# Expert weights fetched by SyncE with a condition instead of by GpSimd's indirect gather, in a two-layer graph-attention and mixture-of-experts kernel

## The chip, the cores and the metric

The kernel runs on one core of a Trainium2 chip. The metric is device time in microseconds (us) of one launch. The engines of the core are TensorE (PE in the profile; its weight loads are PEld), VectorE (DVE), ScalarE (ACT), GpSimd (POOL) and SyncE (SP). SyncE computes nothing here; it begins transfers and holds registers. Each engine works through its own list of instructions in order; semaphores tie the lists together.

## The reference

Two layers run one after the other on `x` (2708 tokens of 256) with a 0/1 matrix `adj` (2708 x 2708). Each layer is a masked attention over the graph with a residual, and then a mixture of 8 experts with a residual:

```python
x = x + gnn0(layernorm(x), adj)          # softmax of masked q k^T / sqrt(d), then elu
x = x + ffn0(layernorm(x))
x = x + gnn1(layernorm(x), adj)          # additive scores, softmax, alpha @ H
x = x + ffn1(layernorm(x))

# ffn0 (hidden size H = 1024); ffn1 is alike with H = 512 and without the norm of its own
probs = softmax(xt @ Wr + br)
top_p, top_idx = top_k(probs, 2)
weights = top_p / top_p.sum(-1)
xe = norm(xt)[None] * ln_g[:, None] + ln_b[:, None]
h = gelu(einsum('end,edh->enh', xe, W1) + b1[:, None])
y = einsum('enh,ehd->end', h, W2) + b2[:, None]
out = (weights * y[top_idx of each token]).sum(over the two experts)
```

Every token uses two of the eight experts, so 5416 rows go through an expert in each layer. All of it is in float32.

## The kernel before

**Stages.** In the trace the first attention ends at about 545 us, the first FFN at 893, the second attention at 1143, the second FFN at 1397; the last scatters and the copy to the output end at 1420.

**Routing.** While attention produces tiles of 128 tokens, each tile is normed and routed: its rows, with the token's number and its gate value appended, are scattered (L748, GpSimd) to a DRAM tensor `disp` that has a region for each expert.

**Slots.** A slot is 128 rows of one expert's region. There are up to 50 slots in a layer; the last four are behind two conditions, and 46 run in the first FFN and 48 in the second. `place` (L755 to L853) works out on VectorE, from the number of rows that each expert has, for every slot: its expert, the first row in `disp` (`token_row`), and where its weights are (`weight_row`). It is called twice in a layer: for the first 24 slots when 16 tiles have been routed, and for the others once all are. 

**Weights.** All the weights and biases of an expert are one packed tensor of 128 rows, one row for each SBUF partition: 17,456 bytes a row (2.23 MB an expert) in the first layer, 9,232 bytes (1.18 MB) in the second. They go into one of `RING = 4` SBUF buffers, slot s into buffer s % 4. Slots of one expert follow each other, so often the buffer holds the wanted expert already from slot s - 4. `fetch_weights` (L872) is a gather by GpSimd (L874) with one row index for each partition; where the buffer has the expert, `place` adds `FAR` to the index, which is then out of bounds, and the transfer of that row is left out.

**Rows.** `fetch_rows` (L882) loads `token_row` into a SyncE register (L884) and moves 128 rows of `disp` to one of six buffers `xg` (L889).

**The loop.** `slot(s)` (in `slots`, L905) runs `up` and then `down` of the slot before:

- `up`: two transposes `tp` (L913, TensorE) of `xg`; a copy to `xe` on VectorE (L917 twice in the first FFN, where it applies the expert's norm, L923 once in the second); a copy of the second bias (L926); the first matmuls `mm` (L933: 16 of them in the first FFN, 8 in the second); gelu on ScalarE (L941) to `hT`.
- `down`: the second matmuls into `acc` (L949: 8 in the first FFN, 4 in the second); then `fetch()` for slot s + `AHEAD`, with `AHEAD = 3`; then `y` on VectorE (L955 adds the bias, L956 multiplies by the gate); then a scatter-add of `y` to the result `xd` in DRAM by GpSimd (L957). The scatter-adds of one layer stand in a chain: each waits for the one before to land, since a token's two rows come from two slots.

Two `ps_mm`, `ps_tp` and `ps_acc` PSUM buffers each, and two buffers of `xe`, `bias2` and `hT`, let two slots overlap.

**What sets the order.** SyncE's list is in the order of the program (`tc.manual_schedule(engines={SP})`). The lists of all other engines are ordered by the scheduler when the program is built, which takes the instructions of all engines together: `up` and `down` are not in the order in which they are written, and a change on one engine can move instructions on another. A `Line` hands out work of the attention stage's last tiles (norms, routing; L682 writes a tile to `xd`) between the steps of the slots.

Of the kernel before, what the change touches and what calls it, by code (L numbers as in the profile page):

```python
# [15 lines left out]
ALU = mybir.AluOpType  # L16
# [3 lines left out]
P = 128  # L20
# [3 lines left out]
E = 8  # L24
# [23 lines left out]
OFTEN = (46, 48)  # L48
AHEAD = 3
DROW = D + 2  # L50
FAR = 1 << 20
IDLE = E * CAP


# [1 line left out]
def adj_ffn_kernel(ctx: ExitStack, tc: tile.TileContext, a: dict, out: bass.AP):  # L56
    nc = tc.nc
# [31 lines left out]
    part = const.tile([P, 1], F32, name="part")  # L89
# [47 lines left out]
    for c in range(DC):  # L137
# [3 lines left out]
            op0=ALU.mult, op1=ALU.mult, accum_out=wfc[:, c, D : D + 1],  # L141
# [471 lines left out]
    class Experts:  # L613
# [141 lines left out]
        def place(self, s0, s1):  # L755
# [3 lines left out]
            all_chunks = s0 > 0  # L759
# [4 lines left out]
            if all_chunks:  # L764
# [3 lines left out]
                for e in range(E):  # L768
                    at = nc.values_load(
                        end[0:1, e : e + 1], min_val=e * CAP, max_val=e * CAP + N,  # L770
                        engines=(mybir.EngineType.SP,),
                        skip_runtime_bounds_check_because="an expert has at most N tokens",
                    )
# [12 lines left out]
            first = one.tile([P, E], F32, name=f"first{s0}")  # L786
# [12 lines left out]
            passed = one.tile([P, n, E], F32, name=f"passed{s0}")  # L799
# [5 lines left out]
            row = one.tile([P, n], F32, name=f"row{s0}")  # L805
# [32 lines left out]
            same = one.tile([P, SLOTS], F32, name=f"same{s0}")  # L838
            r0 = max(s0, RING)
            if s0 < RING:  # L840
# [4 lines left out]
            )  # L845
            weights = one.tile([P, n], F32, name=f"weights{s0}")
            nc.vector.tensor_scalar(
                weights, self.expert[:, s0:s1], float(P), part[:, 0:1], op0=ALU.mult, op1=ALU.add
            )
            nc.vector.scalar_tensor_tensor(  # L850
                self.weight_row[:, s0:s1], same[:, s0:s1], float(FAR), weights,
                op0=ALU.mult, op1=ALU.add,
            )  # L853

        def begin(self):

# [14 lines left out]

        def fetch_weights(self, s):  # L872
            w, packed = self.ring[s % RING], self.packed_weights[0]
            nc.gpsimd.indirect_dma_start(  # L874
                w, None, packed[:],
                bass.IndirectOffsetOnAxis(ap=self.weight_row[:, s : s + 1], axis=0),
                bounds_check=E * P - 1, oob_is_err=False,
            )
            return w

        def fetch_rows(self, s):
# [198 lines left out]
```

The softmax here doesn't subtract the row's maximum and nothing guards it: scores larger than these inputs give would overflow.

## Time and profile before

The kernel takes 1418.33 us (median of 3 runs, 1415.91 to 1423.79). The profiled execution took 1421.76 us, with a span of 1420.0 us and a mean granted TensorE clock of 0.964.

| what | value |
|---|---|
| FFN slots run, first and second | 46 and 48 |
| gathers of weights L874 | 99, mean 1055 ns of GpSimd |
| scatter-adds L957 | 94, mean 1586 ns of GpSimd |
| row transfers L889 | 99 |
| hardware queue q1 (SyncE) | 107.86 MB, 27.0% of 16 DMA engines' time |
| software queue q0 (GpSimd) | 93.73 MB, 23.0% |
| a slot of the first FFN, steady | 7.28 us |
| a slot of the second FFN, without stalls | 4.34 us |

How to read it: PE, DVE, ACT and POOL with a number of us are busy times of an engine over the span. A matmul in float32 leaves two records in the trace, so L949 x1120 are 560 instructions. In lines of costliest groups, "busy, mean ns | idle before, releaser" follow the bar; in a timeline, the columns are start, length, engine, line, operation, `out<-in`, shapes, and in square brackets the idle time before and what ended it. Ends of matmuls are modelled, so neighbours can seem to overlap by 0.1 to 0.2 us.

### The profile page before, as it was taken

The page shows a single profiled execution, that of the slowest core. Times are in us where ns is not written, and L with a number is a line of the kernel's source. Part 1 is how long each engine was busy: PE and PEld are TensorE (multiplying, and loading weights), DVE is VectorE, ACT ScalarE, POOL GpSimd, SP SyncE. Part 2 cuts the span into 40 slices and gives each one's busy share as a digit, 9 for nine tenths or more (in the row PEclk, how much of TensorE's full clock was granted, in tenths as well). Part 3 has the DMA queues.
Part 4 walks back from the last instruction along what each step waited for, and adds up shares of the span by engine and source line. Part 5 has one row for each costly group of instructions (what it writes and reads, how often), then busy time and mean ns, then how long its engine had stood idle before and what let it go on. Part 6 is the DMA issues. An engine that isn't in the chain of part 4 may idle for free. (4 is left out here: it accounts for less than half of the span.)

```text
span 1420.0 us, 21606 instructions
## 1 busy us (share of the span) xinstructions
PE 1292.1 (91%) x7680; PEld 1009.8 (71%) x7680; DVE 569.7 (40%) x2182; ACT 348.9 (25%) x1035; POOL 435.3 (31%) x478
## 2 busy tenths in 40 slices
PE   5999999999999999999999999599989876989872
PEld 3676666666566666999999999478878565878662
DVE  5623744536417264422221222565465543323220
ACT  2322222122112224433333332232001142222120
POOL 5100110110101122543333333431333346555552
PEclk8999999999999999999999999899999978999996
DMA  7601785978727036556686543310221256564664
GB/s 238 207 4 42 205 203 148 248 181 226 190 71 169 23 132 241 156 169 201 203 297 198 155 123 100 81 32 12 65 79 54 73 177 154 114 170 106 183 185 105
DMA packets 108620, 203.01 MB, mean 143 GB/s; under 512 B 25197, under 2 KB 83861, under 8 KB 101933
## 3 DMA queue, kind: packets, MB, share of 16 engines
q1 hardware_dynamic: 76172, 107.86, 27.0%
q0 software_dynamic: 32336, 93.73, 23.0%
q8 instruction: 63, 1.03, 0.3%
q14 instruction: 49, 0.39, 0.1%
HBM read 261.27 MB, written 69.41 MB: 233 GB/s over the span
## 5 line engine op out<-in xcount | busy, mean ns | idle before, releaser
L949 PE MATMUL acc<-ring,hT 128*128 128x256 f32 x1120 | 279.4, 386 | 24.8 <-ACT hT L941 24.8
L933 PE MATMUL mm<-xe,ring 128*128 128x128 f32 x2240 | 286.0, 283 | 9.7 <-DVE xe L923 4.7
L933 PEld LDWEIGHTS mm<-xe,ring 128*128 128x128 f32 x2240 | 275.9, 198 | 23.9 <-issue 14.0
L941 ACT ACTIVATE hT<-mm,ring 128x128 f32<-128x128 f32 x560 | 159.6, 368 | 376.8 <-issue 292.7
L949 PEld LDWEIGHTS acc<-ring,hT 128*128 128x128 f32 x1120 | 200.0, 192 | 55.9 <-ACT hT L941 34.6
L345 PE MATMUL s<-g,xnT 128*128 128x512 f32 (+1 forms) x440 | 215.2, 605 | 4.9 <-DVE mT L357 4.9
L367 PE MATMUL acc<-v,p 128*128 128x257 f32 (+1 forms) x880 | 216.9, 390 | 0.0
L957 POOL DMA_INDIRECT xd<-y,xg x94 | 149.1, 1586 | 173.5 <-DVE y L955 61.1
L517 PE MATMUL acc<-parts,mT 128*128 128x257 bf16 (+1 forms) x1452 | 175.7, 274 | 1.5 <-POOL parts L504 1.0
L955 DVE TENSOR_TENSOR y<-acc,bias 128x256 f32<-128x256 f32 x94 | 39.8, 424 | 339.1 <-PE acc L949 286.6
L367 PEld LDWEIGHTS acc<-v,p 128*128 128x128 f32 (+1 forms) x880 | 159.7, 192 | 19.2
L517 PEld LDWEIGHTS <-mT 128*128 128x128 fp8e4 (+1 forms) x1452 | 137.4, 98 | 30.6 <-issue 9.7
L748 POOL DMA_INDIRECT disp<-row,to x88 | 86.4, 982 | 235.7 <-DVE to L745 139.2
L874 POOL DMA_INDIRECT ring<-L_ffn_packed,weight_row x99 | 104.4, 1055 | 157.9 <-issue 102.9
L156 POOL TENSOR_TENSOR ln_rs<-ln_rs,minus_half 128x2 f32<-128x2 f32 x88 | 66.8, 779 | 245.9 <-DVE ln_rs L152 198.6
L357 DVE TENSOR_SCALAR mT<-s 128x512 fp8e4<-128x512 f32 x110 | 75.4, 687 | 150.4 <-ACT p L356 149.2
L345 PEld LDWEIGHTS s<-g,xnT 128*128 128x128 f32 (+1 forms) x440 | 77.1, 187 | 58.4 <-issue 45.9
L356 ACT ACTIVATE p<-s 128x512 f32<-128x512 f32 x110 | 65.0, 594 | 192.3 <-PE s L351 192.3
L351 PEld LDWEIGHTS <-apart 128*128 128x128 fp8e4 (+1 forms) x440 | 34.2, 99 | 64.5 <-issue 64.5
L257 DVE TENSOR_SCALAR apart<-adj 128x677 fp8e4<-128x677 int32 x80 | 40.9, 515 | 54.2 <-DMA adj<-in_adj_dram 53.7
L913 PE MATMUL tp<-ident,xg 128*128 128x128 f32 x188 | 39.3, 279 | 20.3 <-DMA xg<-disp 17.2
L166 PE MATMUL misc<-ident,xn 128*128 128x128 f32 (+1 forms) x132 | 27.5, 290 | 23.4 <-DVE ln_rs L152 11.6
(183 smaller groups left out, 1067.7 us busy)
## 6 DMA issues: line engine op xcount, KB each, us to landing
adj<-in_adj_dram SPq DMA_DIRECT2D x84, 338.5 KB
L_ffn_packed<-in_L_ffn_W_dram SPq DMA_DIRECT2D x16, 1024.0 KB
xg<-disp SPq DMA_DIRECT2D x99, 129.0 KB
L_ffn_packed<-in_L_ffn_W_dram SPq DMA_DIRECT2D x16, 512.0 KB
neighbours<-mT SPq DMA_DIRECT2D x5, 1408.0 KB
mT<-neighbours SPq DMA_DIRECT2D x5, 1408.0 KB
xin<-in_x_dram SPq DMA_DIRECT2D x42, 128.0 KB
xd<-x SPq DMA_DIRECT2D x42, 128.0 KB
```

Source lines behind the costliest of these rows:

```text
L156: nc.gpsimd.tensor_tensor(rs[:r, 1], rs[:r, 0], minus_half[:r], ALU.pow)
L345: nc.tensor.matmul(ps[:kr, :nb], xnT[:, c, k0 : k0 + kr], g[:, c, :nb], start=(c == 0), stop=False,)
L356: nc.scalar.activation(p[:kr, :nb], ps[:kr, :nb], AF.Exp, scale=1.0 / 16.0)
L357: nc.vector.tensor_scalar(mT[:kr, k, :], ps[:kr, :nb], -BIG / 2, None, ALU.is_gt, saturate=False,)
L367: nc.tensor.matmul(accs[j][:r], p[:kr, j * P : j * P + r], v[:kr, k, :], start=(k == 0), stop=(k == NT - 1),)
L517: nc.tensor.matmul(acc[:r], mT[:, k, q0 : q0 + r], parts[:, k, i], start=(k == 0 and i == 0), stop=(k == NT - 1 and i == 2),)
L748: nc.gpsimd.indirect_dma_start(disp[:], bass.IndirectOffsetOnAxis(ap=to[:r, j : j + 1], axis=0), rows2[j][:r], None,)
L874: nc.gpsimd.indirect_dma_start(w, None, packed[:], bass.IndirectOffsetOnAxis(ap=self.weight_row[:, s : s + 1], axis=0), bounds_check=E * P ...
L933: nc.tensor.matmul(ps[:, i, :], w[:, c * hidden + f * P : c * hidden + (f + 1) * P], xe[:, c, :], start=(c == 0), stop=(c == DC - 1),)
L941: nc.scalar.activation(hT[:, f, :], ps[:, i, :], AF.Gelu, bias=w[:, b1 + f : b1 + f + 1])
L949: nc.tensor.matmul(ps, hT[:, f, :], w[:, w2 + f * D : w2 + (f + 1) * D], start=(f == 0), stop=(f == hc - 1),)
L957: start = nc.gpsimd.indirect_dma_start(xd[:], bass.IndirectOffsetOnAxis(ap=xg.bitcast(I32)[:, D : D + 1], axis=0), y, None, compute_op=ALU ...
```

## The change

The weights of a slot are fetched by SyncE in place of GpSimd. `place` now writes `weight_row` as twice the first row of the expert in the packed tensor, plus one where the buffer has the expert already (or, in the second call, where the slot is past the last one in use). SyncE loads that number into a register, shifts it for the row, and begins an ordinary transfer of 128 rows with the lowest bit as its condition. The gather, its list of 128 indices and `FAR` go. It is meant to free GpSimd, whose other work in the slots is the chain of scatter-adds, and to take the weights out of GpSimd's software queue. `fetch()` calls `fetch_weights` and then `fetch_rows`, as before, so on SyncE the weights of slot s + 3 now stand ahead of its rows.

```diff
@@ place
             weights = one.tile([P, n], F32, name=f"weights{s0}")
             nc.vector.tensor_scalar(
-                weights, self.expert[:, s0:s1], float(P), part[:, 0:1], op0=ALU.mult, op1=ALU.add
-            )
-            nc.vector.scalar_tensor_tensor(
-                self.weight_row[:, s0:s1], same[:, s0:s1], float(FAR), weights,
-                op0=ALU.mult, op1=ALU.add,
-            )
+                weights, self.expert[:, s0:s1], float(E - 1), float(2 * P), op0=ALU.min, op1=ALU.mult
+            )
+            if all_chunks:
+                nc.vector.tensor_tensor(
+                    same[:, s0:s1], same[:, s0:s1], passed[:, :, E - 1], ALU.max
+                )
+            nc.vector.tensor_add(self.weight_row[:, s0:s1], same[:, s0:s1], weights)
@@ fetch_weights
             w, packed = self.ring[s % RING], self.packed_weights[0]
-            nc.gpsimd.indirect_dma_start(
-                w, None, packed[:],
-                bass.IndirectOffsetOnAxis(ap=self.weight_row[:, s : s + 1], axis=0),
-                bounds_check=E * P - 1, oob_is_err=False,
-            )
+            at = nc.values_load(
+                self.weight_row[0:1, s : s + 1], min_val=0, max_val=2 * (E * P - P) + 1,
+                engines=(mybir.EngineType.SP,),
+                ...
+            )
+            row = nc.s_assert_within(
+                at >> 1, 0, E * P - P,
+                ...
+            )
+            nc.sync.dma_start(w, packed[bass.ds(row, P), :], cond=(at & 1) == 0)
             return w
```

## The prediction

> **What bounds the kernel now.** I read the page first: busy shares, then the 40 slices.
>
> ```profile
> PE 1292.1 (91%) x7680; PEld 1009.8 (71%) x7680; DVE 569.7 (40%) x2182; ACT 348.9 (25%) x1035; POOL 435.3 (31%) x478
> ...
> PE   5999999999999999999999999599989876989872
> ```
>
> TensorE (PE) is at 9 tenths or more nearly everywhere; each slice is 35.5 us. Only slices 31 to 40 (from about 1100 us, the second FFN) have holes. So the change must be judged in two stages with different limits. The windows by stage confirm it (columns: window, length, PE, PEld, DVE, ACT, POOL busy, PE clock, DMA share, GB/s): the first FFN, then the second.
>
> ```profile
> 600.00:700.00 100.00, 100.00 (x690) 92.20 (x689) 20.75 (x65) 31.93 (x112) 35.97 (x28) 1.00 0.63 193
> 700.00:800.00 100.00, 100.00 (x693) 92.12 (x692) 22.11 (x70) 30.78 (x108) 35.08 (x27) 1.00 0.71 231
> ```
>
> ```profile
> 1250.00:1300.00 50.00, 42.83 (x265) 37.16 (x265) 15.45 (x41) 11.85 (x42) 26.07 (x21) 0.97 0.63 172
> ```
>
> The first FFN has no TensorE hole at all: nothing removed from GpSimd can help it, and anything that opens a hole costs its full length. The second has 14% idle. Its waits, PE alone, 1190 to 1405 us (total, times, longest):
>
> ```profile
> PE acc L949 <- ACT hT L941: 24.2, 40, 10.6
> PE tp L913 <- DMA xg<-disp: 8.8, 5, 2.8
> PE mm L933 <- DMA ring<-L_ffn_packed,weight_row: 4.7, 4, 1.4
> ```
>
> The long one is not a wait for gelu alone: all engines stop for some 10 us near 1180. Rows and weights together cost 13.5 us.
>
> What the removed instruction cost GpSimd is in the costliest groups:
>
> ```profile
> L874 POOL DMA_INDIRECT ring<-L_ffn_packed,weight_row x99 | 104.4, 1055 | 157.9 <-issue 102.9
> L957 POOL DMA_INDIRECT xd<-y,xg x94 | 149.1, 1586 | 173.5 <-DVE y L955 61.1
> ```
>
> GpSimd is 31% busy, so these 104 us are not a bound by themselves.
>
> **What hides the transposes.** The timeline of one first-FFN slot on TensorE (start, length, engine, line; 7.28 us from tp to tp):
>
> ```profile
> 853.14 0.38 PE L913 MATMUL tp<-ident,xg 128*128 128x128 f32 x2
> 853.36 1.03 PE L949 MATMUL acc<-ring,hT 128*128 128x256 f32 x4
> 854.22 0.64 PE L933 MATMUL mm<-xe,ring 128*128 128x128 f32 x4
> 854.70 0.60 PE L949 MATMUL acc<-ring,hT 128*128 128x256 f32 x2
> 855.13 3.29 PE L933 MATMUL mm<-xe,ring 128*128 128x128 f32 x28
> ```
>
> The first mm needs xe, which VectorE copies out of tp, and comes 1.08 us after tp's start. Those are filled by two matmuls of the down of the slot before (s, where tp belongs to s+1) (1.03 us; four records, two to an instruction, as everywhere in this trace).
>
> **What the Trainium skill says.** "DMA: Bandwidth & Descriptors", section "Issuing engines are not separate DMA queues", says that DMAs begun by SyncE or GpSimd run on the same 16 engines and interleave, so another issuer saves sequencer time only. The trace agrees as far as it goes: hardware and software queues both do their bytes there (27.0% and 23.0% of 16 engines' time for 107.86 and 93.73 MB, about equal cost a byte). So the moved weights land at about the old rate. Same page, "Latency and other measured facts": first byte after about 600 ns for SyncE's path and 1 us for GpSimd's; the trace shows GpSimd busy 1.055 us for one gather and no first byte. I take 0.4 us saved per transfer, which nothing waits for in steady state.
>
> **The change part by part.**
>
> *GpSimd*: 99 x 1.055 = 104.4 us go. In the first FFN they lie beside a full TensorE: 0. In the second a gather sits between two scatter-adds. Each scatter waits for the one before to land: starts 4.55 to 6 us apart, mean about 5.1 over 40 of them. TensorE's slot is 4.34 us where it doesn't stall (tp at 1240.38, mm from 1242.99, 4.34 or 4.39 apart) but 4.83 on average (slot 7's mm at 1193.71, slot 45's at 1377.33: 183.6/38). This is the relief to be had: at most 38 x (4.83 - 4.34) = 18.6 us, with a few more at both ends.
>
> *SyncE*: per fetch one more register load, two register operations, and a DMA. The trace has a register load at 0.19 us and a row DMA at 0.33 us median, a register operation at 0.04; with a margin for the condition 0.75 us, 99 x 0.75 = 74 us. SyncE has nothing else in the slots but rows, whose wait on a freed xg is 415.6 us in all: hidden. What is new is order. The row's load stands behind the weights, and those wait for the down that frees the ring buffer; but that down is the same point of the program that issued the gather before, and both are wanted three slots later (13 us in the second FFN, over 20 in the first). I take 0, and 10 us as the upper end, for attention's last tiles, whose xd writes stand on the same engine.
>
> *Skipping*: about as many transfers are skipped as now; bytes unchanged: 0.
>
> *VectorE in place*: one operation more, twice a layer, small: under 0.5 us.
>
> *Order of matmuls*: the part that the diff doesn't show. Only SyncE's order is written out; the rest is set when the program is built, and moving 99 instructions off GpSimd changes it. I compared the two built instruction lists on TensorE. Slots of the first FFN:
>
> ```
> before: mm x14 | down(s-1) x5 | tp(s+1) x2 | down(s) x2 | mm(s+1) x2 | down(s) x1 | mm x14
> after:  mm(s) x16 | down(s) x8 | tp(s+1) x2 | mm(s+1) x16
> ```
>
> Before, 41 of 50 boundaries have two downs between tp and the mm that needs it; after, 35 have none, 5 one, 8 two, 2 three. On VectorE y of the finished down now stands ahead of xe, often with the bias copy too. In the second FFN tp stood between mm and down, filling part of the gelu wait (at 1240.38 tp, at 1241.05 down, after 0.29 idle); after, 41 of 50 are mm, down, tp, mm.
>
> Price in the first FFN: with nothing between, TensorE stands from tp's start to the first mm with 1.08 us, of which tp's own 0.2 to 0.38 was paid before; but the downs that filled 1.03 us come elsewhere, so a slot grows by 1.03. With one down between (0.5 us) about 0.6. Where y and both others go first, 0.34 + 0.28 more. Over 46 slots: 0.70 x 46 x 1.07 = 34, plus 5 x 0.6 = 3, plus some 3 for the longer VectorE orders: **+40 us** (30 to 52).
>
> Price in the second: mm start to down start stays 2.46 (1238.59 to 1241.05, gelu ends that), down start to tp 1.83 (1241.05 to 1242.88), then tp to mm: y from 0.20 to 0.62, xe pitched 0.34 behind it and 0.42 long, 0.1 to the matmul, 1.1. Sum 5.4 where it was 4.34 stall-free. The stalls on rows and weights should vanish, since a slot is longer than everything behind it (scatter 4.55). Against 4.83: 38 x 0.57 = 22, less some boundaries with the old order, **+18 us** (0 to 30).
>
> *Ends of the second FFN*: slots 46 and 47 and the last scatters (1394.27, 1399.68, 1404.24) run behind today by two slots; without gathers between them -9. Start: rows arrive beside three gathers and TensorE waits up to 5.46 us at 1139.35; GpSimd stands 11.42 us at 1155.50 before a gather while the last tiles' norm is behind it; -5 of these. **-14 us** (-25 to 0).
>
> Sum: 1418.3 + 40 + 18 - 14 = 1462, taken as 1460.
>
> **Rivals.**
> *GpSimd relief wins* (0.13): the copies' exposure is small, because TensorE's queue runs at a modelled end and weight loads overlap; first FFN +10, second at 4.4 a slot, -16, ends -14: 1398. For: 14% holes in the second FFN; GpSimd 52% busy there against 36% in the first. Against: 1.08 us from tp to mm are measured, and a strict engine order can't fill them.
> *No change* (0.07): half the exposure, 20, against -20: 1418. It needs two errors that cancel.
> *SyncE becomes a second brake* (0.20): the longer VectorE order in all slots (1.6 exposed: 46 x 1.6 = 74 less what is filled, some 60), and rows that wait behind a weight's buffer (+10), gains as above: 1418 + 60 + 10 + 18 - 14 = 1492. For: SyncE's waits can't be passed by what stands behind. Against: three slots of slack.
> *Forecast* (0.60): 1460.
>
> **How the numbers follow.** Faster by over 0.5% is the first rival, 0.13; within, 0.07; slower is the forecast and the last, 0.80. The forecast's own bounds: 1418 + 30 + 0 - 25 = 1423 to 1418 + 52 + 30 - 0 = 1500, ends seldom met together. The range keeps no change (1418) and all but the upper third of the last rival, so it leaves out 0.13 and 0.07: 1416 to 1494.
>
> **What would show it.** First FFN: PE in windows of 100 us falls from 100 to about 88, the slot grows from 7.28 to about 8.3 us, and a wait of mm on xe appears in nearly every slot, some 0.7 us each, for 30 us or more. Second FFN: slot about 5.4 us, waits on xg and ring almost gone, waits on xe up to 30 us. Attention unchanged within 3 us; POOL busy about 331 us. It is wrong if PE in the first FFN stays at 100, or if the second FFN is shorter than its 254 us (1143 to 1397); the SyncE rival is right if waits for rows or ring exceed 20 us.

## The result, and the profile after

The changed kernel takes 1452.97 us (median of 4 runs, 1451.25 to 1455.37) against 1417.12 us for the kernel before on the same chip: 1.0246 times as long, with a 95% interval of 1.0207 to 1.0286. That is 36 us slower; 1460 was forecast. The two profiled executions that are compared below differ by 30 us, since the one before took 1421.76 us, 4.6 more than its median.

The page of the changed kernel, its busy shares and the slices of TensorE:

```profile
PE 1302.6 (90%) x7680; PEld 1011.0 (70%) x7680; DVE 561.9 (39%) x2184; ACT 346.5 (24%) x1033; POOL 327.8 (23%) x379
...
PE   5999999999999999999999999699989977777873
```

GpSimd lost 107.5 us of work, as it was to. TensorE has the same 7680 matmul records; its share hardly moved, and the tenths of the slices are too coarse to show the loss. The windows show it (window, length, then PE, PEld, DVE, ACT, POOL busy, PE clock, DMA share, GB/s), two of the first FFN and one of the second:

```profile
600.00:700.00 100.00, 92.27 (x612) 83.82 (x611) 20.71 (x63) 27.56 (x98) 21.65 (x14) 1.00 0.58 178
700.00:800.00 100.00, 94.29 (x631) 85.66 (x630) 20.82 (x65) 27.64 (x98) 19.69 (x13) 1.00 0.67 210
...
1250.00:1300.00 50.00, 40.32 (x244) 33.73 (x244) 11.25 (x37) 10.92 (x39) 14.03 (x9) 1.00 0.54 143
```

TensorE stood at 100 of 100 us in the first FFN before; now it has 6 to 8 us of holes in 100 and 9 to 11% fewer matmul records in the same time. What ended the holes is in the waits of TensorE, whole run:

```profile
PE mm L938 <- DVE xe L928: 26.3, 38, 1.7
PE mm L938 <- DVE xe L922: 22.5, 30, 1.5
PE acc L954 <- ACT hT L946: 21.5, 40, 1.8
...
PE tp L918 <- DMA xg<-disp: 2.6, 1, 2.6
...
PE mm L938 <- DMA ring<-L_ffn_packed: 1.5, 2, 1.3
```

The two first lines are new in this size: `mm` waits for the copy `xe` in the second FFN (L928, 38 times) and in the first (L922, 30 times). The waits for rows and weights, 17.2 and 4.7 us before, fell to 2.6 and 1.5. One slot of the first FFN on TensorE's timeline has the reason in it:

```profile
879.80 3.84 PE L938 MATMUL mm<-xe,ring 128*128 128x128 f32 x32 [0.62 <-DVE xe L922]
883.48 3.62 PE L954 MATMUL acc<-ring,hT 128*128 128x256 f32 x16
886.93 0.38 PE L918 MATMUL tp<-ident,xg 128*128 128x128 f32 x2
887.93 3.84 PE L938 MATMUL mm<-xe,ring 128*128 128x128 f32 x32 [0.62 <-DVE xe L922]
```

Nothing stands between `tp` at 886.93 and the `mm` at 887.93 that needs its copy. From `mm` to `mm` are 8.13 us where it was 7.28. Of the 45 boundaries between slots of the first FFN, one had `mm` right behind `tp` in the trace before; 30 have it now. Added up by stage, from the first `mm` to the last `acc` of each FFN on TensorE (us):

| stage | before | after | difference |
|---|---|---|---|
| up to the first FFN's first mm | 552.8 | 552.3 | -0.5 |
| first FFN | 340.4 | 367.4 | +27.0 |
| rest of the second attention, to the second FFN's first mm | 250.5 | 245.3 | -5.2 |
| second FFN | 253.7 | 265.2 | +11.5 |
| last scatters and copy | 22.6 | 19.8 | -2.8 |
| span | 1420.0 | 1450.0 | +30.0 |

### The profile page after: what moved, and what is told of

Read it like the earlier page. It is cut to its first block, busy times and chain, and to the rows that moved or that the text cites. A ratio compares the mean times of both kernels' runs of the same rounds, so it can differ in the third digit from the quotient of the medians.

```text
span 1450.0 us, 21996 instructions
## 1 busy us (share of the span) xinstructions
PE 1302.6 (90%) x7680; PEld 1011.0 (70%) x7680; DVE 561.9 (39%) x2184; ACT 346.5 (24%) x1033; POOL 327.8 (23%) x379
## 3 DMA queue, kind: packets, MB, share of 16 engines
q8 instruction: 63, 1.03, 0.3%
## 5 line engine op out<-in xcount | busy, mean ns | idle before, releaser
L938 PE MATMUL mm<-xe,ring 128*128 128x128 f32 x2240 | 278.1, 281 | 50.9 <-DVE xe L928 26.3
L938 PEld LDWEIGHTS mm<-xe,ring 128*128 128x128 f32 x2240 | 262.7, 194 | 71.7 <-DVE xe L928 36.4
L954 PE MATMUL acc<-ring,hT 128*128 128x256 f32 x1120 | 268.2, 386 | 21.7 <-ACT hT L946 21.5
L946 ACT ACTIVATE hT<-mm,ring 128x128 f32<-128x128 f32 x560 | 159.3, 368 | 424.0 <-issue 383.8
L954 PEld LDWEIGHTS acc<-ring,hT 128*128 128x128 f32 x1120 | 204.1, 191 | 54.1 <-ACT hT L946 31.3
L922 DVE TENSOR_SCALAR xe<-tp,ring 128x128 f32<-128x128 f32 x92 | 33.6, 401 | 60.8 <-PE tp L918 60.8
L350 PE MATMUL s<-minus_big,apart 128*128 128x128 bf16 (+1 forms) x440 | 42.8, 220 | 0.0
```

Source lines behind the costliest of these rows:

```text
L350: nc.tensor.matmul(ps[:kr, j * P : j * P + r], apart[:, j, k0 : k0 + kr], minus_big[:, :r], start=False, stop=(j == len(ts_) - 1),)
L938: nc.tensor.matmul(ps[:, i, :], w[:, c * hidden + f * P : c * hidden + (f + 1) * P], xe[:, c, :], start=(c == 0), stop=(c == DC - 1),)
L946: nc.scalar.activation(hT[:, f, :], ps[:, i, :], AF.Gelu, bias=w[:, b1 + f : b1 + f + 1])
L954: nc.tensor.matmul(ps, hT[:, f, :], w[:, w2 + f * D : w2 + (f + 1) * D], start=(f == 0), stop=(f == hc - 1),)
```

## Experiments

Each kernel ran beside the kernel before on the same chip; a time is followed by its ratio to that kernel and, in brackets, the 95% interval of the ratio. Four theories are named in the expectations. **A**: the loss is the order of matmuls that the rebuilt program got. **B**: it is the fetch by SyncE itself. The first four kernels tell these apart, two orders by two ways to fetch. They also brought a result that neither foresaw, and **C** (a weight transfer of SyncE delays the landing of the scatter-add beside it) and **D** (SyncE's instructions and waits do it) are about that.

### Two orders by two ways to fetch

In all four, TensorE's list in the slots is tied down by edges from each of its matmuls to the one before, and `down` is split so that its matmuls are written between or ahead of `up`'s. Nothing else is written differently; the lists of the other engines are again ordered by the scheduler. The comments in the cut are not in the kernels.

```diff
-                hT, bias2 = up(w, xg)
+                xe, bias2 = up_tp(w, xg)                 # tpfirst: tp, down, mm
+                ps = None if behind is None else down_mm(*behind)
+                hT = up_mm(w, xe)                        # downfirst has down_mm ahead of up_tp
 ...
+            def behind_in_list(i):                       # called on every matmul of up and down
+                if pe:
+                    tc.add_manual_dep(i.ins, pe[0].ins.name, ..., reason="order")
+                pe[:] = [i]
```

**The kernel before with the common order of the changed one** (gather_downfirst):

> The kernel before, gathers on GpSimd untouched, with the order of the changed kernel's common slot tied down in all slots: mm(s), down(s), tp(s+1), mm(s+1). Theory A: the loss appears without any change to the fetch: first-FFN slots 8.13 us (46 x 0.85 = +39), second-FFN slots 5.4 us where they averaged 4.83 (+18), stalls on rows and weights gone, start and end as before: about 1470 us. Theory B: within 10 us of the kernel before, 1410 to 1428 us.

Measured: 1485.42 us, 1.0428 of the kernel before (1.0401 to 1.0455), 15 us over the 1470 expected. The first FFN took 383.8 us (+43.4) and the second 290.1 (+36.4). The slots of the second FFN are 5.40 us apart from slot 6 to slot 45, as expected; what is over in this stage lies at its two ends, mostly before slot 7. The gathers on GpSimd were untouched, and the slot has the same hole, as TensorE's timeline shows:

```profile
863.31 0.38 PE L927 MATMUL tp<-ident,xg 128*128 128x128 f32 x2
864.31 3.93 PE L951 MATMUL mm<-xe,ring 128*128 128x128 f32 x32 [0.62 <-DVE xe L932]
```

So the order alone makes a loss of this kind, without the change to the fetch. This is against theory B.

**The changed kernel with that order in all slots** (sync_downfirst):

> The changed kernel with mm(s), down(s), tp(s+1), mm(s+1) in all slots, where the built order has about 7 in 10 of them. Theory A: first-FFN slots all 8.13 us, 46 x 0.85 = 39 against the 29 us lost now, the second FFN as now at 5.40: about 1463 us, and 7 us below the gathers with this order (the start's row waits). Theory B: no more than 3 us from the changed kernel, 1450 to 1456 us.

Measured: 1479.34 us, 1.0399 (1.0369 to 1.0429). The first FFN took 382.6 us, 1 us from the gathers with this order. With this order the fetch makes no difference in the first FFN; the order makes all of it. The time came out 16 us above what was expected. Some 10 us of that lie in the second FFN, which took 275.1 us where the changed kernel has 265.2, and 5 in the first, whose slots took 8.22 us for 8.13; the kernel before took 1423.42 us beside it, 6 us more than beside the changed kernel. Against the gathers with the same order, this second FFN is 15 us shorter. Both kernels take 205 us from slot 7 to slot 45, so SyncE's fetch gains at the ends of the second FFN, as the prediction has it.

**The kernel before with the transposes first** (gather_tpfirst):

> The kernel before, gathers on GpSimd untouched, with mm(s), tp(s+1), down(s), mm(s+1) tied down in both FFNs. It prices the fetch alone against the changed kernel with the same order. Theory A: first-FFN slots stay 7.28 us; the second FFN keeps its stalls for rows and weights and its scatter-adds 5.1 us apart, 4.8 us a slot: 1405 to 1420 us, and 15 to 25 us above the changed kernel with this order. Theory B: at or below the changed kernel with this order.

Measured: 1424.21 us, 0.9998 (0.9977 to 1.002). The first FFN took 340.9 us, the second 259.9. This order and the order built for the kernel before are worth the same in total time. The other half of the expectation was missed: this kernel is 19 us below the changed kernel with the same order, the next one, where theory A had it 15 to 25 us above. On that side theory B was right.

**The changed kernel with the transposes first** (sync_tpfirst):

> The changed kernel, with TensorE's order in the slot loops tied down: mm(s), tp(s+1), all of down(s), mm(s+1), in both FFNs. Theory A, the loss is the order of matmuls that the rebuilt program got: first-FFN slots 7.28 us again (-29 us over the stage), second-FFN slots 4.34 to 4.55 us (down to what the scatter-adds allow, 37 x 0.9 = -33), so about 1391 us, below both kernels, with the waits of mm on xe gone. Theory B, the loss is the fetch by SyncE itself (weights and rows landing later, or SyncE's order): slots stay near 8 and 5.4 us, 1440 to 1455 us, and TensorE waits for ring or xg where it waited for xe.

Measured: 1443.61 us, 1.0135 (1.0109 to 1.0161), some 50 us above what theory A expected. It lies in the range of theory B, but without B's signs: slots of the first FFN didn't stay near 8 us, and TensorE waits 39.8 us for `xe` in the second FFN and only 11.1 for `ring` and `xg`. The first FFN did as theory A said: slots of 7.25 us, 345.5 us in all. TensorE's timeline there:

```profile
872.30 0.38 PE L932 MATMUL tp<-ident,xg 128*128 128x128 f32 x2
872.52 3.62 PE L972 MATMUL acc<-ring,hT 128*128 128x256 f32 x16
875.98 3.73 PE L956 MATMUL mm<-xe,ring 128*128 128x128 f32 x32
```

The second FFN did not: 278.3 us, where the kernel before took 253.7 and the changed one 265.2. From 1195 to 1247 us its slots ran 4.29 us apart, and then between 4.5 and 8 us. In that part VectorE waits like this (its waits, 1245 to 1405 us):

```profile
DVE y L982 <- DMA xd<-y,xg: 118.1, 25, 7.0
```

`y` needs one of three buffers, which an earlier scatter-add has to leave, and while VectorE stands there it makes no `xe` for TensorE: a `tp` of 1268.25 us got its `xe` at 1273.24, behind a `y` that was let go at 1272.31. So the chain of scatter-adds bounds this stage once TensorE is fast. Theory B has a part in it after all, but in a place that the changed kernel doesn't show. GpSimd's timeline of the same kernel:

```profile
1265.58 1.61 POOL L984 DMA_INDIRECT xd<-y,xg  x1 [5.49 <-DVE y L982]
1272.94 1.61 POOL L984 DMA_INDIRECT xd<-y,xg  x1 [5.75 <-DVE y L982]
1280.30 1.61 POOL L984 DMA_INDIRECT xd<-y,xg  x1 [5.75 <-DVE y L982]
1284.85 1.61 POOL L984 DMA_INDIRECT xd<-y,xg  x1 [2.94 <-DVE y L982]
1289.44 1.63 POOL L984 DMA_INDIRECT xd<-y,xg  x1 [2.99 <-DVE y L982]
```

The brackets name `y`, but this `y` is for a later slot, since its second instruction ended only at 1273.12, behind the start of the scatter-add at 1272.94: one landing lets go both the next scatter-add and the `y` that takes the freed buffer. Starts are 7.4, 7.4, 4.6 and 4.6 us apart. The bytes of the hardware queue tell which is which. First the DMA view from 1272.94 to 1280.30, then from 1280.30 to 1284.85 (queue, packets, MB, share of 16 engines):

```profile
q1 hardware_dynamic: 288, 1.31, 54.8%
q0 software_dynamic: 144, 0.13, 11.4%
```

```profile
q0 software_dynamic: 144, 0.13, 27.0%
q1 hardware_dynamic: 144, 0.13, 11.1%
```

In the long interval a weight transfer (1.18 MB) was beside the scatter-add's 0.13 MB; in the short one there were only rows. From 1213 us to the end, 14 intervals are longer than 6 us and sum to 103.7 us, 40 us more than 14 of 4.55 would be. Of the intervals between 1240 and 1410 us, the 13 with a weight transfer in them are 7.1 to 8.3 us, and 14 of the 16 without one are 4.5 to 4.6.

### What delays the scatter-adds

These kernels start from sync_tpfirst.

**No weight transfers in the second FFN after slot 3** (sync_tp_noload):

```diff
+            if self.hidden == 512:
+                nc.vector.memset(same[:, r0:s1], 1.0)
```

> The kernel sync_tpfirst with every weight transfer of the second FFN after slot 3 skipped by its condition (SyncE's instructions stay): it leaves out those weights, so its slots use stale ones. Theory C, a weight transfer begun by SyncE shares the DMA engines with the scatter-add just issued and delays its landing, and the chain of scatter-adds is the bound: scatter-adds 4.5 to 4.6 us apart throughout, no waits of y for landings over 1 us each, 37 us less, about 1406 us. Theory D, SyncE's own instructions or the wait for freed xg buffers slow the chain: starts stay 7 us apart in places and the time within 10 us of sync_tpfirst.

Measured: one run, 1388.48 us beside 1411.94 for the kernel before, 0.983. The second FFN took 230.4 us for 278.3, so 48 us less; 37 less were expected. GpSimd's timeline; from 1230 us on all starts but two are 4.3 to 4.6 us behind the last:

```profile
1271.32 1.55 POOL L986 DMA_INDIRECT xd<-y,xg  x1 [2.96 <-issue]
1275.69 1.55 POOL L986 DMA_INDIRECT xd<-y,xg  x1 [2.82 <-issue]
1280.10 1.55 POOL L986 DMA_INDIRECT xd<-y,xg  x1 [2.86 <-issue]
1284.60 1.55 POOL L986 DMA_INDIRECT xd<-y,xg  x1 [2.95 <-issue]
```

SyncE's loads, shifts and skipped transfers are all still there. So theory D is out as the main cause, and C holds in this: it is the transfer itself that delays the landing.

**Weights in four transfers of a quarter of the columns** (sync_tp_split4):

```diff
-            nc.sync.dma_start(w, packed[bass.ds(row, P), :], cond=(at & 1) == 0)
+            part = self.packed_weights[-1] // 4
+            for c in range(0, 4 * part, part):
+                nc.sync.dma_start(
+                    w[:, c : c + part], packed[bass.ds(row, P), c : c + part], cond=(at & 1) == 0
+                )
```

> The kernel sync_tpfirst with a slot's weights moved as four transfers of a quarter of the columns (2,308 bytes a row in the second FFN, 4,364 in the first, for 9,232 and 17,456). Theory C with sharing packet by packet: a scatter-add's packets wait behind packets a quarter as long, so scatter-adds with a transfer beside them start about 5.5 us apart where it was 7.2, 14 x 1.7 = 24 us less, about 1419 us. If only the bytes in flight count, and not the packets' size: no change, 1438 to 1446 us. Theory D: slower, by four times the issues on SyncE.

Measured: 1423.39 us, 1.0083 (1.005 to 1.0116) against 1.0135 whole; the second FFN 266.2 us. GpSimd's timeline, with a transfer beside each of the last two:

```profile
1256.30 1.54 POOL L988 DMA_INDIRECT xd<-y,xg  x1 [4.74 <-issue]
1262.58 1.60 POOL L988 DMA_INDIRECT xd<-y,xg  x1 [4.74 <-DVE y L986]
1269.08 1.60 POOL L988 DMA_INDIRECT xd<-y,xg  x1 [4.89 <-DVE y L986]
```

6.3 and 6.5 us apart: less than 7.4, more than the 5.5 expected. The ratio fell by 0.005, about 7 us, where 24 were expected. The same bytes in four transfers of shorter packets hold a scatter-add up less; but about two thirds of the delay stay (1.9 us over 4.55, where it was 2.8), so the packet's length is at most a part of it. The number of transfers changed along with the length, and no run tells the two apart. The Trainium skill, "DMA: Bandwidth & Descriptors", section "SWDGE vs HWDGE vs iDMA", says that the two kinds of queue feed different internal queues of an engine, which goes round-robin between them. The two kernels, with whole and with quartered transfers, agree with that in direction; no run here shows the turns themselves.

**Ten row buffers for six** (sync_tp_xg10):

```diff
-            xg = self.one.tile([P, DROW], F32, name="xg", bufs=RING + 2)
+            xg = self.one.tile([P, DROW], F32, name="xg", bufs=RING + 6)
```

> The kernel sync_tpfirst with ten xg buffers for six, so SyncE doesn't stand at a row fetch until a scatter-add lands, and the next slot's weights aren't begun just as the next scatter-add is. Theory C: contention stays wherever the transfer begins, since a transfer lasts about as long as a scatter-add's landing; between -12 and +3 us, 1431 to 1447 us. Theory D, it is SyncE's wait and the alignment that it makes: transfers move away from the scatter-adds, starts 4.6 to 5 us apart, 1405 to 1420 us.

Measured: 1425.29 us, 1.0108 (1.0063 to 1.0153); the second FFN 266.4 us. Its interval overlaps that of sync_tpfirst, so a gain is not shown by the times. In sync_tpfirst each weight transfer between 1240 and 1410 us moves its first packet 1.4 to 1.8 us behind the start of a scatter-add; here it is anywhere from 0.3 to 6.6 us. Scatter-adds with a transfer beside them still start 6.2 to 8.0 us apart, so the delay stays when the transfer begins at another moment, as C has it, and not the 4.6 to 5 that D expected. It is shorter in some places than the 7.1 to 8.3 of sync_tpfirst, so the moment has some part.

**The same register and condition, begun by GpSimd in its software queue** (pool_tp):

```diff
-                engines=(mybir.EngineType.SP,),
+                engines=(mybir.EngineType.Pool,),
-            nc.sync.dma_start(w, packed[bass.ds(row, P), :], cond=(at & 1) == 0)
+            nc.gpsimd.dma_start(w, packed[bass.ds(row, P), :], cond=(at & 1) == 0)
```

> The kernel sync_tpfirst with the same register, shift and condition, but GpSimd as the engine that loads the register and begins the weights' transfer, as a plain one in its software queue. Theory C: in the scatter-adds' own queue the transfer follows the scatter-add issued before it and lies in the gap before the next, as the gathers did: starts with a transfer between them 5.2 to 5.6 us apart, 1415 to 1425 us, as gather_tpfirst. Theory D (the register, the shift and the condition cost, whichever engine runs them): near 1440 us.

Measured: 1420.7 us, 1.0054 (1.0036 to 1.0072); the second FFN 258.7 us, for 278.3 on SyncE. The register and the condition are the same, so they don't cost the 20 us. What changed is the queue, and with it the moment at which the transfer begins. With ten row buffers that moment moved too, and the second FFN still took 266.4 us, so most of it is put down to the queue; the two are not fully told apart. Long intervals are 5.3 to 6.8 us here, and 5.1 to 5.7 for the most part with the gathers. GpSimd's timeline of gather_tpfirst:

```profile
1317.72 1.61 POOL L979 DMA_INDIRECT xd<-y,xg  x1 [1.58 <-DVE y L977]
1319.63 1.06 POOL L874 DMA_INDIRECT ring<-L_ffn_packed,weight_row  x1 [0.30 <-issue]
1323.13 1.60 POOL L979 DMA_INDIRECT xd<-y,xg  x1 [2.44 <-DVE y L977]
```

The gather is issued 1.9 us behind the scatter-add, into the same queue, and 1.16 MB, the scatter-add's 0.13 among them, moved in that queue between the two starts; they still start 5.4 us apart, not 7.4.

### Does the changed kernel pay for this too?

**The changed kernel, built order, no weight transfers in the second FFN after slot 3** (after_noload; the same two lines as above):

> The changed kernel in its built order, with every weight transfer of the second FFN after slot 3 skipped by its condition: it leaves out those weights. TensorE's list is the same as the changed kernel's. If the slow order hides the transfers' effect on the scatter-adds there: second-FFN slots still 5.40 us, and at most 5 us less than the changed kernel, 1.021 to 1.027 of the kernel before. If the transfers cost the changed kernel time as well: 15 us less or more, 1.013 or below.

Measured: one run, 1453.48 us beside 1423.71, 1.0209, at the lower end of the interval of the changed kernel. The second FFN took 264.4 us for 265.2, with slots 5.40 us apart. The changed kernel doesn't pay. In its second FFN, `y` on VectorE waits for TensorE alone and not once for a scatter-add, where sync_tpfirst had 118.1 us of that (VectorE's waits in the changed kernel, 1165 to 1430 us):

```profile
DVE y L960 <- PE acc L954: 163.3, 42, 7.0
```

The transfers delay the scatter-adds there too: 12 of them have a transfer beside them between 1240 and 1410 us, which begins 0.2 to 5.9 us behind the start of a scatter-add, and start 5.2 to 8.5 us apart. But those without one mostly start 4.4 to 4.8 us apart and catch up, so the mean over both is 5.35 us from 1200 us on, just within TensorE's slot. So the slow order hides a delay that shows as soon as the order is repaired.

### Both ways to fetch in one kernel

**Gathers, transposes first, the first three slots' weights by SyncE** (hybrid_tp):

```diff
+            if s < AHEAD:
+                at = nc.values_load(self.weight_row[0:1, s : s + 1], ..., engines=(mybir.EngineType.SP,), ...)
+                nc.sync.dma_start(w, packed[bass.ds(at, P), :])
+                return w
             nc.gpsimd.indirect_dma_start(
```

> The kernel gather_tpfirst with the weights of the first three slots of each FFN begun by SyncE behind the rows, and all later ones gathered by GpSimd into its own queue. If SyncE's gain lies at the second FFN's start and its loss in the scatter-adds' landing: slot 0 to slot 1 of the second FFN 8.5 us or less where it was 13.3, scatter-adds with a weight transfer between them 5.2 to 5.6 us apart, 5 to 10 us less than gather_tpfirst: 0.993 to 0.997 of the kernel before. If the start's gain is only shifted into the chain of scatter-adds: 0.998 to 1.002.

Measured: 1417.38 us beside 1423.71, 0.9956 (0.9939 to 0.9973), the only kernel here that does all the work and is shown to be faster than the kernel before. The gain is 6 us of 1424. TensorE's waits for weights in the second FFN are gone, but waits for `xe` stand in their place (waits of TensorE, gather_tpfirst and then hybrid_tp):

```profile
PE mm L951 <- DMA ring<-L_ffn_packed,weight_row: 17.6, 11, 3.1
```

```profile
PE mm L959 <- DVE xe L946: 21.1, 13, 3.0
```

Slot 0's and slot 1's first mm are 9.1 us apart, over the 8.5 expected, where they were 14.4, but slot 0 itself came 4 us later. Scatter-adds with a weight transfer between them start 5.0 to 6.9 us apart. The gain is as large as expected; that it comes from the start, as expected, is not shown.

## Why the prediction was right

- **Where the loss is.** The prediction put it in the order of the matmuls and mostly in the first FFN. The stages show +27.0 of +30.0 us there, and gather_downfirst shows the same loss with the old fetch.
- **First FFN, +40 (30 to 52).** Measured +27.0, below this range: the mechanism was right and a term too large. The fill that is lost was read as 1.03 us from the timeline, which includes the modelled end of the last matmul (start to start it is 0.86 there), and the sum then took 1.07. A boundary with nothing between costs 8.13 - 7.28 = 0.85 us. Of the 38 boundaries from slot 7 on, 22 cost that; six cost more, at 8.6 to 9.0 us a slot, and in the trace of such a slot VectorE puts all of `y` and the bias copy ahead of `xe`, as was feared; the ten with one or two of `down`'s matmuls between cost only 0.2 each. Together they are +29.2, the first seven +0.2, and the last slot ends 2.4 earlier. Slots of 8.22 us in the two tied-down kernels have the same hole of 0.62 us; where their other 0.09 comes from is not shown.
- **Second FFN.** The slot of 5.40 us was forecast as 5.4. Here the sum was right, since it went from start to start and left modelled ends out. VectorE's timeline shows the steps that it was made of, `y` and then `xe`:

```profile
1257.32 0.42 DVE L960 TENSOR_TENSOR y<-acc,bias 128x256 f32<-128x256 f32 x1 [4.18 <-PE acc L954]
1257.66 0.41 DVE L928 COPY xe<-tp 128x256 f32<-128x256 f32 x1
```

- **+18 for slots and -14 for both ends** of the second FFN. From slot 7 to slot 45 the traces have 203.4 us for 183.6: +19.8. All else outside the first FFN is -16.8: about -10 in the second attention and up to slot 7, where -5 was forecast, and -6 behind slot 45, where -9 was. Both parts are in their ranges, so the forecast didn't come near by errors that cancel; it missed by the first FFN's term.
- **Signs that were named.** PE in a window of 100 us was to fall to about 88: 92 to 94. Waits on `xe` of some 0.7 us: 0.62, 30 times, 22.5 us where 30 were named. POOL at 331: 327.8. Waits for rows and weights under 20 us: 4.1. The register load priced at 0.19 us was the shortest in the trace; the median there is 0.27. It changed nothing, since SyncE's work is hidden.
- **The weights "land at about the old rate", 0.** This stood in the sum without harm, and is where the reasoning had a hole. The transfers do land soon enough; what the step left out is what they do to the scatter-adds. That it did no harm is luck: the chain was reckoned at 4.55 us a scatter-add, and with the delays it ran at 5.35, just under the slot of 5.40. With the transposes first the same transfers cost about 18 us (sync_tpfirst against gather_tpfirst, 278.3 against 259.9 us in the second FFN). The Trainium skill, "DMA: Bandwidth & Descriptors", section "Issuing engines are not separate DMA queues", says that another issuer only saves time on the sequencer. Here the choice of queue also changed when another transfer lands, and the measurement decides.
- **The rivals.** Relief of GpSimd is not to be had: the chain of scatter-adds is bound by landings, not by GpSimd's time (1.55 us of the 4.5 between two starts without transfers). SyncE as a second brake was thought of as waits on its own list. SyncE does stand 367.8 us for `ring` buffers, but TensorE waits only 4.1 us for rows and weights; where a brake of SyncE showed, with the transposes first, it was the delay of the scatter-adds.

What is open: why the build chose another order when the gathers left GpSimd was not tried; the lists only show that it did. In the lines above `y` starts 0.34 us ahead of `xe` on VectorE; whether `xe` first would close part of the hole, with TensorE's order as it is, was not tried. How much of the scatter-adds' delay is packets and how much bytes was tried at two lengths only, and which shared part of the path makes them wait is not shown.

## What to carry to other kernels

Before pricing a change, compare the orders in which the two programs were built: moving an instruction from one engine to another can come with a new order on a third one. TensorE was 100% busy here, and a transpose with nothing behind it until its copy was done cost 0.85 us, once for each slot. Where a chain of small transfers sets a stage's end, ask of every large transfer which queue it is in and what is in flight beside it, not only whether it lands in time. Tie down an order that you need; then test the change again under that order, since a slow order can hide a second cost.

## What the runs showed of the hardware that was not expected

- A scatter-add of 128 rows of 1 KB starts 4.3 to 4.6 us behind the one before it, for the most part, if it has to wait for that to land, and nothing large is in flight (sync_tp_noload).
- A 1.18 MB transfer begun by SyncE beside it makes that 7.1 to 8.3 us with rows of 9,232 bytes (sync_tpfirst; 5.2 to 8.5 in the changed kernel, where it begins at other moments), and 6.1 to 6.6 for the most part with quarters of 2,308 bytes (sync_tp_split4). The same bytes gathered by GpSimd into the queue of the scatter-adds make it 5.1 to 5.7 for the most part (gather_tpfirst; 3 of 12 are 6.3 to 7.3).
- A conditional transfer takes little of SyncE itself: in the changed kernel its issue, skipped or done, has a median of 84 ns (99 times, at most 358), beside a register load with a median of 272 ns.
